# Row numbers of a graph scatter from a scan and two narrow matmuls, and four PSUM banks for the edge rows

## The chip, the cores and the metric

The kernel runs on one core of a Trainium2 chip. The metric is the device time of one execution in microseconds (us). The times are medians over several executions; lower is better.

## The reference, cut to what matters

A graph layer with 6250 nodes of 64 features and 206,250 directed edges (100,000 in both directions and one loop per node), sorted by `dst`. `W1a` to `Wr` are small dense weights, the hidden width is 128.

```
msg  = concat([x[dst], edge_attr], axis=1)          # 206250 x 128
h    = relu(msg @ W1a.T + b1a) @ W1b.T + b1b
sums = segment_sum(h, src, 6250);  counts = segment_sum(1, src, 6250)
agg  = sums / max(counts, 1)
z    = relu(concat([x, agg]) @ W2a.T + b2a) @ W2b.T + b2b
out  = concat([z, x]) @ Wr.T + br
return layernorm(x + out)
```

Edges come in the order of `dst`, but are summed by `src`. Between the two the rows of all edges have to be brought into another order.

## The kernel before

All of the timed work is in `fast_path`. The edges are padded to 1612 tiles of 128 and taken in 124 groups of 13 tiles (`NGR`, `NG`, `BLK`). The nodes are divided into 49 bins of 128 consecutive `src` numbers (`NB`; padded to 50, `2 * HALF`). Each edge row is sent to a place in a DRAM table `rows`, within the region of its bin; later the table is read back bin by bin, and a one-hot matmul sums the rows of each bin. There are five epochs (`EPOCHS`: 82, 17, 14, 7 and 4 groups), each with a table, and within the first one several steps, after which the part of the table that is then full can be read.

One turn of the main loop, `for k, ep_ in enumerate(epoch_of)`, does this, and each step is written for the engines in this order:

1. `group(k + 3)`: SyncE loads edge features (L700), the place of each edge's `dst` in a window (L912), and the window's table `ytab` (L918), into one of four `rhs` buffers.
2. ScalarE copies the low seven bits of `src` into the rows of the group (L1182).
3. `counts_of` (L850, L851) for group k + 1: four TensorE matmuls into two PSUM banks, `cnt_ps`.
4. `hidden(k, ...)` for tiles 0 to 9 in parts of 4, 3 and 3: TensorE multiplies (L949) into an `h_ps` bank, ScalarE applies Relu and writes the rows `orow` (L950; five buffers). An f32 product is two passes in the trace.
5. `columns(k + 2)` (L929) and `bins_of(k + 2)` (L830, L831, L837) on VectorE.
6. In turns 6 to 18, `nodes_ahead` (L1150 to L1160), work of the node layer that needs no sums.
7. `issue(k)`: SyncE reads back parts of the table into one of nine `rt` buffers (`READS`, L1005).
8. `sum_next()`, if sums are due: VectorE makes one-hots of the next reads (L1031, L1034), TensorE multiplies them with the rows (L1050, into one of two `sum_ps` banks), VectorE adds the result to `part` (L1106).
9. `slots(k + 1)` (L867, L872): VectorE writes the row numbers `rowidx` of group k + 1.
10. `hidden(k, ((10, 3),))`, the last three tiles, after the first two sums.
11. `scatter(k)`: GpSimd issues 13 indirect DMAs (L956), each of 128 rows of 130 numbers, to the places that `rowidx` names.

TensorE, VectorE, ScalarE and SyncE run in exactly the order in which the program is written (`manual_schedule`). After the loop the last bins are summed and the node layer follows. GpSimd has no part in that.

How a row number is found before the change: `bins_of` compares the bin number of each edge with 0 to 49, which gives a one-hot of 50 bins x 13 tiles for each partition, with a column 0 ahead of each bin that holds what that partition and bin had up to the previous group (L830). A running sum over it (L837, the scan) numbers the edges within partition and bin; only differences within a bin matter. `counts_of` adds up the 128 partitions: `one_w` sums the counts of all partitions, `before_w` adds those of the partitions below in the same tile, and `BIG` on the diagonal marks the bin that the edge belongs to. `slots` takes the maximum over the 50 bins (L867), which is the marked one, and adds the bin's start (L872).

PSUM has eight banks: one holds the constants `ramp`, `in_win` and `on` that VectorE reads, two are `cnt_ps`, two `sum_ps` and three `h_ps`.

Of the kernel before, what the change touches and what calls it, by code (L numbers as in the profile page):

```python
# [8 lines left out]
F32 = mybir.dt.float32  # L9
# [454 lines left out]
ROWS, EDGES, READS = 5, 4, 9  # L464
# [13 lines left out]
def fast_path(  # L478
# [161 lines left out]
    eye_b = const.tile([P, P], F32, name="eye_b")  # L640
    nc.vector.tensor_scalar(eye_b, diff_i, 0.0, BIG, op0=ALU.is_equal, op1=ALU.mult)
# [36 lines left out]
    with (  # L678
# [6 lines left out]
        tc.tile_pool(name="hps", bufs=3, space=PSUM) as hp,  # L685
# [10 lines left out]
        rhss = [rp.tile([P, NG * P], F32, name=f"rhs{i}") for i in range(EDGES)]  # L696

# [28 lines left out]
        def y_rows(b_lo, b_hi):  # L726
            for b0 in range(b_lo, b_hi, SUB):
                n = min(SUB, b_hi - b0)
                ps = hp.tile([P, SUB, H], F32, name="h_ps")
                for j in range(n):  # L730
                    b = b0 + j
                    nc.tensor.matmul(
                        ps[:, j, :], zT[: D + 1, b * P : (b + 1) * P], w1x_t, start=True, stop=True
                    )
                nc.scalar.copy(part[:, b0 : b0 + n, :H], ps[:, :n, :])
                if b0 + n == NB or (b0 + n) % (4 * SUB) == 0:
                    c0 = b0 // (4 * SUB) * (4 * SUB)
                    nc.scalar.dma_start(yv[:, c0 : b0 + n, :], part[:, c0 : b0 + n, :H])
# [17 lines left out]
        nc.vector.scalar_tensor_tensor(  # L756
            before_w, diff_i, 0.0, eye_b, op0=ALU.is_gt, op1=ALU.add
        )
        state = {"rt": 0, "bad": 3}
# [5 lines left out]
        none_b = const.tile([P, 2 * HALF], BF16, name="none_b")  # L765
        nc.vector.memset(none_b, 0.0)
# [52 lines left out]
        hads = {}  # L819

        def bins_of(k):


            ep_ = epoch_of[k]
            c0 = k * BLK
            oh = slp.tile([P, 2 * HALF * T], BF16, name="bins")
            had = slp.tile([P, 2 * HALF * T], BF16, name="had")
            by_bin = oh.rearrange("p (b t) -> p b t", t=T)
            was = none_b if k == ep_.first else state["had"][:, :, BLK]
            nc.vector.tensor_tensor(by_bin[:, :, 0], was, on.rearrange("p (b t) -> p b t", t=T)[:, :, 1], op=ALU.mult)  # L830
            nc.vector.tensor_tensor(  # L831
                by_bin[:, :, 1:],
                ramp[:, : 2 * HALF, None].to_broadcast([P, 2 * HALF, BLK]),
                hi[:, None, c0 : c0 + BLK].to_broadcast([P, 2 * HALF, BLK]),
                op=ALU.is_equal,
            )
            nc.vector.tensor_tensor_scan(had, on, oh, 0.0, op0=ALU.mult, op1=ALU.add)  # L837
            oh, had = (v.rearrange("p (b t) -> p b t", t=T) for v in (oh, had))
            state["had"] = hads[k] = had
            return oh, had  # L840

        def counts_of(oh, had):

            ps = slpp.tile([P, 2, 512], F32, name="cnt_ps")
            for i in range(2):
                v = ps[:, i, : HALF * T].rearrange("p (b t) -> p b t", t=T)
                b = slice(i * HALF, (i + 1) * HALF)
                nc.tensor.matmul(v, one_w, had[:, b, :], start=True, stop=False)  # L850
                nc.tensor.matmul(v[:, :, :BLK], before_w, oh[:, b, 1:], start=False, stop=True)  # L851
            return ps

        def slots(k, ps):

            ep_ = epoch_of[k]
            c0 = k * BLK
            at = (k - ep_.first) % SEG * BLK
            if at == 0:
                m = min(ep_.end - k, SEG) * BLK  # L860
                state["bin"] = slp1.tile([P, SEG * BLK], F32, name="bin_at")[:, :m]
                nc.vector.tensor_scalar(
                    state["bin"], hi[:, c0 : c0 + m], float(STRIDE), -BIG, op0=ALU.mult, op1=ALU.add
                )
            v = ps[:, :, : HALF * T].rearrange("p i (b t) -> p i b t", t=T)
            row = slp.tile([P, T], F32, name="row")
            nc.vector.tensor_reduce(row, v.rearrange("p i b t -> p t i b"), axis=mybir.AxisListType.XY, op=ALU.max)  # L867

            def by_now(t):
                nc.vector.tensor_copy(t.rearrange("p (i b) -> p i b", i=2), v[:, :, :, BLK])  # L870

            s = nc.vector.scalar_tensor_tensor(  # L872
                rowidx[:, c0 : c0 + BLK], row[:, :BLK], BIG + STRIDE - 1,
                state["bin"][:, at : at + BLK], op0=ALU.min, op1=ALU.add,
            )
            state["slots"] = s.ins
            if k + 1 == EARLY:
                by_now(early)
                wrong(early, epochs[0].low, ALU.is_gt, slp)
            for st in ep_.steps[:-1]:  # L880
                if k + 1 == st.at:
                    full = slp1.tile([P, 2 * HALF], F32, name="full")
                    by_now(full)
                    wrong(full, st.hi, ALU.is_lt, slp)
            if k + 1 == ep_.end:
                by_now(ep_.tot)
                unused(ep_)

                if (ep_.end - ep_.first) * BLK > 255:
                    most = slp.tile([P, 2 * HALF], F32, name="most")  # L890
                    nc.vector.tensor_scalar(
                        most, hads[k][:, :, BLK], 255.5, None, op0=ALU.is_gt, op1=ALU.add,
                        accum_out=bad[:, state["bad"] :][:, :1],
                    )
                    state["bad"] += 1
# [38 lines left out]
        def window(g):  # L934

            ps = hp.tile([P, H], F32, name="h_ps")
            nc.tensor.matmul(ps[D:, :], near[: D + 1, g, :], w1x_t, start=True, stop=True)
            nc.scalar.copy(mv[g % MV][D:, :], ps[D:, :])
# [3 lines left out]
        def hidden(k, parts):  # L942
            orow = orows[k % ROWS]
            rhs, _, m = made[k]
            for k0, n in parts:
                ps = hp.tile([P, SUB, H], F32, name="h_ps")
                for j in range(n):
                    c = k0 + j
                    nc.tensor.matmul(ps[:, j, :], rhs[:, c * P : (c + 1) * P], m, start=True, stop=True)  # L949
                nc.scalar.activation(orow[:, k0 : k0 + n, :H], ps[:, :n, :], AF.Relu)  # L950
# [195 lines left out]
        def nodes_ahead(b0):  # L1146
            n = min(SUB, NB - b0)
            cols = slice(b0 * P, (b0 + n) * P)
            qp = hp.tile([P, SUB * P], F32, name="h_ps")
            nc.tensor.matmul(qp[:, : n * P], w2x_t, zT[: D + 1, cols], start=True, stop=True)  # L1150
            xp = hp.tile([P, 2, SUB, D], F32, name="h_ps")
            for j in range(n):
                b = slice((b0 + j) * P, (b0 + j + 1) * P)
                nc.tensor.matmul(xp[:, 0, j, :], zT[: D + 1, b], wrx_t, start=True, stop=True)  # L1154
            nc.vector.tensor_scalar(nq[:, cols], qp[:, : n * P], -1.0, None, op0=ALU.mult)  # L1155
            nc.scalar.copy(xr[:, b0 : b0 + n, :], xp[:, 0, :n, :])
            for j in range(n):
                b = slice((b0 + j) * P, (b0 + j + 1) * P)
                nc.tensor.matmul(xp[:, 1, j, :], nq[:, b], nwzz_t, start=True, stop=True)  # L1159
            nc.vector.tensor_add(xr[:, b0 : b0 + n, :], xr[:, b0 : b0 + n, :], xp[:, 1, :n, :])  # L1160
# [12 lines left out]
        counts = counts_of(*bins_of(0))  # L1173
        columns(0)
        slots(0, counts)
        for k, ep_ in enumerate(epoch_of):
# [6 lines left out]
            if k == 0:  # L1183
                hidden(k, ((0, 4), (4, 3), (7, 3), (10, 3)))
                window(1)
                columns(1)
                ahead = bins_of(1)
            if k + 1 < NGR:
                counts = counts_of(*ahead)
# [8 lines left out]
            if k + 2 < NGR:  # L1198
                columns(k + 2)
                ahead = bins_of(k + 2)  # L1200
# [17 lines left out]
            if k == 4:  # L1218


                wps = hp.tile([P, P], F32, name="h_ps")
# [3 lines left out]
                wps = hp.tile([P, D], F32, name="h_ps")  # L1225
# [5 lines left out]
                wps = hp.tile([P, H + D], F32, name="h_ps")  # L1231
# [11 lines left out]
            for i in range(max(due, 1)):  # L1243
# [3 lines left out]
                if i == 0 and k + 1 < NGR:  # L1247
                    slots(k + 1, counts)
# [23 lines left out]
        with tc.tile_pool(name="nw", bufs=3) as nw:  # L1272

            class Nodes:
# [17 lines left out]
                def turned(self):  # L1292
                    tr = hp.tile([P, SUMS * P], F32, name="h_ps")
# [5 lines left out]
                def layer(self):  # L1299
                    p1 = hp.tile([P, SUMS * P], F32, name="h_ps")[:, : self.nb * P]  # L1300
# [3 lines left out]
                def residual(self):  # L1304
                    p3 = hp.tile([P, SUMS, D], F32, name="h_ps")
# [65 lines left out]
            bad_ps = slpp.tile([P, NBAD], F32, name="cnt_ps")  # L1371
# [61 lines left out]
```

## Time and profile before

| what | value |
|---|---|
| median of 16 runs | 2555.23 us (2540.46 to 2564.58) |
| the profiled execution | 2554.95 us |
| its span in the trace | 2553.2 us |
| mean granted TensorE clock | 0.718 of full speed |
| scatter L956: instructions, busy | 1612, 1547.8 us |
| first scatter starts, last scatter starts | 17.5 us, 2428.0 us |
| DMA traffic | 375.2 MB, 147 GB/s |

Line numbers (L956) are those of the kernel before. PE is TensorE's matmul, PEld its weight load, DVE is VectorE, ACT ScalarE, POOL GpSimd, and SPq SyncE's DMA queue. A group row of the page gives line, engine, operation, output and inputs, shape and count; then busy us and mean ns of one; then the engine's idle time just before these instructions, with what ended most of it. "issue" is idle time in which the engine waited for nothing that the profile shows; "remote" is a wait whose end the profile can't lay to an instruction of this core.

### The profile page before, as it was taken

To read this page: it belongs to the slowest core of one execution; us is meant where nothing else is said; L and a number is where in the kernel's file an instruction comes from. 1 tells how busy PE (TensorE), PEld (TensorE's weight loads), DVE (VectorE), ACT (ScalarE), POOL (GpSimd) and SP (SyncE) were. 2 spreads that over 40 slices of the span, in tenths; PEclk is the share of its full clock that TensorE was granted. 3 is DMA by queue.
4 is the path that set the end of the run, shared out by engine and by line. 5 is a ranking of instruction groups with operands and counts; after the bars stand their busy time and mean duration, and the time that the engine had idled before them with its cause. 6 is when DMAs were issued, how large, how long until landed. Compare 5 with 4: busy or idle time off the path is not lost.

```text
span 2553.2 us, 25025 instructions
## 1 busy us (share of the span) xinstructions
PE 1442.2 (56%) x8253; PEld 1269.4 (50%) x8253; DVE 1186.9 (46%) x1993; ACT 325.7 (13%) x807; POOL 1555.7 (61%) x1630
## 2 busy tenths in 40 slices
PE   3645462345554554445545566665666565665796
PEld 2534452344444444435444456555555564565795
DVE  5333343333433544333444555464555454554587
ACT  1211110111111111001101001110111100110106
POOL 6666566666666666666666666656666666666500
PEclk7665665666776776667776777777777776787898
DMA  6657554534444444334444444644445454555581
GB/s 162 192 193 263 156 156 127 181 114 127 125 126 126 124 132 116 116 105 128 129 130 121 141 153 148 182 131 133 151 134 169 146 146 141 164 163 158 173 259 37
DMA packets 198783, 375.21 MB, mean 147 GB/s; under 512 B 47098, under 2 KB 113980, under 8 KB 198516
## 3 DMA queue, kind: packets, MB, share of 16 engines
q1 hardware_dynamic: 121314, 223.67, 31.2%
q0 software_dynamic: 51584, 107.40, 13.2%
q10 hardware_dynamic: 25746, 42.45, 4.9%
q8 instruction: 67, 1.10, 0.2%
q14 instruction: 72, 0.59, 0.1%
HBM read 221.77 MB, written 151.59 MB: 146 GB/s over the span
## 4 chain that ended last, share of the span: by engine, by line
PE 20%; issue 12%; another core or an unknown queue 11%; DVE 5%; ACT 1%; SPq 1%; DMA 1%; ACTq 0%; DVEq 0%
PE sum_ps L1050 12%; PE h_ps L949 7%; DVE oh L1034 2%; DVE part L1106 1%; PE cnt_ps L850 1%; PE cnt_ps L851 1%; DVE rhs L929 1%; DMA rhs<-in_edgeT 1%; SPq L1005 1%; DVE had L837 1%; ACT orow L950 0%; ACT agg L1288 0%; DMA rt<-rows 0%; DVE row L867 0%
## 5 line engine op out<-in xcount | busy, mean ns | idle before, releaser
L956 POOL DMA_INDIRECT rows<-orow,rowidx x1612 | 1547.8, 960 | 872.6 <-issue 453.8
L949 PE MATMUL h_ps<-mv,rhs 128*128 128x128 f32 x3224 | 639.5, 349 | 477.2 <-issue 342.0
L949 PEld LDWEIGHTS h_ps<-mv,rhs 128*128 128x128 f32 x3224 | 574.9, 257 | 549.2 <-issue 398.1
L1050 PE MATMUL sum_ps<-rt,oh 128*128 128x129 f32 x4006 | 609.4, 310 | 264.2 <-issue 230.7
L1050 PEld LDWEIGHTS sum_ps<-rt,oh 128*128 128x128 f32 x4006 | 577.0, 225 | 287.1 <-issue 249.6
L950 ACT ACTIVATE orow<-h_ps 128x512 f32<-128x512 f32 x496 | 247.2, 519 | 2043.7 <-remote 1395.5
L1034 DVE TENSOR_TENSOR oh<-ramp,rt 128x512 f32<-128x512 f32 (+3 forms) x213 | 147.4, 704 | 595.1 <-DMA rt<-rows 430.6
L929 DVE TENSOR_TENSOR rhs<-rhs,ramp 64x1664 f32<-64x1664 bf16 x116 | 219.4, 1891 | 28.8 <-DMA rhs<-relt 14.0
L850 PE MATMUL cnt_ps<-had,one_w 128*128 128x350 bf16 x248 | 98.6, 400 | 186.5 <-issue 113.8
L837 DVE TENSOR_TENSOR_SCAN had<-ramp,bins 128x700 bf16<-128x700 bf16 x124 | 200.3, 1615 | 4.2
L1034 DVE TENSOR_TENSOR oh<-ramp,node 128x512 f32<-128x512 f32 (+3 forms) x237 | 187.4, 791 | 8.0
L1106 DVE TENSOR_TENSOR part<-part,sum_ps 128x258 f32<-128x258 f32 (+2 forms) x183 | 86.2, 472 | 214.0 <-remote 153.9
L867 DVE TENSOR_REDUCE row<-cnt_ps 128x14 f32<-128x700 f32 x124 | 109.1, 880 | 111.1 <-remote 64.0
L851 PEld LDWEIGHTS <-before_w 128*128 128x128 bf16 x248 | 28.4, 115 | 210.9 <-issue 199.5
L1031 DVE SCALAR_TENSOR_TENSOR node<-unused,rt 128x4 f32<-128x4 bf16 (+3 forms) x237 | 37.8, 159 | 184.2 <-DMA rt<-rows 125.6
L851 PE MATMUL cnt_ps<-bins,before_w 128*128 128x325 bf16 x248 | 100.7, 408 | 28.3 <-issue 28.3
L831 DVE TENSOR_TENSOR bins<-ramp,hi 128x650 bf16<-128x650 f32 x124 | 108.3, 873 | 0.0
L1155 DVE TENSOR_SCALAR zT<-h_ps 128x512 f32<-128x512 f32 (+1 forms) x13 | 8.6, 661 | 132.8 <-PE h_ps L1154 74.5
L1150 PE MATMUL h_ps<-zT,w2x_t 65*128 65x512 f32 (+1 forms) x26 | 21.7, 931 | 64.4 <-ACT orow L950 53.0
L850 PEld LDWEIGHTS <-one_w 128*128 128x128 bf16 x248 | 29.6, 119 | 56.0 <-issue 45.9
L830 DVE TENSOR_TENSOR bins<-had,ramp 128x50 bf16<-128x50 bf16 x119 | 44.2, 371 | 2.7
L1159 PE MATMUL h_ps<-nwzz_t,zT 128*128 128x64 f32 x98 | 22.3, 402 | 40.6 <-DVE zT L1155 34.9
(113 smaller groups left out, 395.9 us busy)
## 6 DMA issues: line engine op xcount, KB each, us to landing
rt<-rows SPq DMA_DIRECT2D x242, 260.0 KB
rhs<-in_edgeT SPq DMA_DIRECT2D x124, 416.0 KB
rt<-rows SPq DMA_DIRECT2D x106, 390.0 KB
rows<-orow,rowidx POOLq DMA_INDIRECT x1612
rhs<-relt SPq DMA_DIRECT2D x116, 208.0 KB
rows<-padrow ACTq DMA_DIRECT2D x4, 4680.0 KB
rows<-padrow ACTq DMA_DIRECT2D x8, 2340.0 KB
rt<-rows SPq DMA_DIRECT2D x48, 325.0 KB
```

The source lines that it names most:

```text
L831: nc.vector.tensor_tensor(by_bin[:, :, 1:], ramp[:, : 2 * HALF, None].to_broadcast([P, 2 * HALF, BLK]), hi[:, None, c0 : c0 + BLK].to_broa ...
L837: nc.vector.tensor_tensor_scan(had, on, oh, 0.0, op0=ALU.mult, op1=ALU.add)
L850: nc.tensor.matmul(v, one_w, had[:, b, :], start=True, stop=False)
L851: nc.tensor.matmul(v[:, :, :BLK], before_w, oh[:, b, 1:], start=False, stop=True)
L867: nc.vector.tensor_reduce(row, v.rearrange("p i b t -> p t i b"), axis=mybir.AxisListType.XY, op=ALU.max)
L929: nc.vector.tensor_tensor(rhs[D:, :].rearrange("p (h e) -> p h e", h=2), rel, in_win[D:, :, None].to_broadcast([WIN, 2, NG * P // 2]), op= ...
L949: nc.tensor.matmul(ps[:, j, :], rhs[:, c * P : (c + 1) * P], m, start=True, stop=True)
L950: nc.scalar.activation(orow[:, k0 : k0 + n, :H], ps[:, :n, :], AF.Relu)
L956: s = nc.gpsimd.indirect_dma_start(out=ep_.rows, out_offset=bass.IndirectOffsetOnAxis(ap=rowidx[:, t : t + 1], axis=0), in_=orow[:, j, :], ...
L1034: nc.vector.tensor_tensor(res[:, at_tile : at_tile + nb * n, :], ramp[:, None, :].to_broadcast([P, nb * n, P]), node[:, :, None].to_broadc ...
L1050: nc.tensor.matmul(of_bin(b), oh[:, at_tile, :], rt[:, j * n + t, : H + 1], start=t0 + t == st.lo[b], stop=t0 + t == st.hi[b] - 1,)
L1106: nc.vector.tensor_add(to, to, g.ps[:, : g.nb, :])
```

## The change

The row number is put together differently, and PSUM is divided differently.

- `bins_of` writes the one-hot into one of two fixed buffers `ohs`, whose column 0 stays zero. The scan then numbers within partition, bin and group (`nth`). A new 50-column VectorE operation adds the last column to a running count, `had` (L848 of the kernel after).
- `counts_of` is replaced by `bases_of` (L885, L886 after): two matmuls of 50 columns, one that sums the counts of all partitions over the groups before, and one that adds the partitions below in this group. `counted` (L858 after) adds a third matmul in the eleven turns in which the totals are needed.
- `slots` adds `bases` (PSUM) to `nth` (SBUF) over 128 x 650 numbers (L900 after), adds `BIG` where the one-hot is set (L903 after, both inputs in SBUF), takes the maximum over the bins of an SBUF tile (L905 after), and adds the bin's start (L906 after).
- `cnt_ps` becomes one bank. `h_ps` becomes four single banks that `bank()` hands out in turn. The parts of a group stay at 4, 3, 3 and 3 tiles. `nodes_ahead` uses three banks where it used two.
- `READS` goes from 9 to 8. `eye_b` and `none_b` are no longer needed.

```diff
-ROWS, EDGES, READS = 5, 4, 9
+ROWS, EDGES, READS = 5, 4, 8
...
-        tc.tile_pool(name="hps", bufs=3, space=PSUM) as hp,
+        tc.tile_pool(name="hps", bufs=1, space=PSUM) as hp,
...
+        banks = hp.tile([P, 4, 512], F32, name="h_ps")
+        def bank(n=1):
+            i = -(-state["bank"] // n) * n % 4
+            state["bank"] = (i + n) % 4
+            return banks[:, i : i + n, :].rearrange("p i f -> p (i f)")
...
         def bins_of(k):
-            was = none_b if k == ep_.first else state["had"][:, :, BLK]
-            nc.vector.tensor_tensor(by_bin[:, :, 0], was, on.rearrange("p (b t) -> p b t", t=T)[:, :, 1], op=ALU.mult)
             nc.vector.tensor_tensor(
-                by_bin[:, :, 1:],
+                ohs[k % 2][:, :, 1:],
                 ramp[:, : 2 * HALF, None].to_broadcast([P, 2 * HALF, BLK]),
                 hi[:, None, c0 : c0 + BLK].to_broadcast([P, 2 * HALF, BLK]),
                 op=ALU.is_equal,
             )
-            nc.vector.tensor_tensor_scan(had, on, oh, 0.0, op0=ALU.mult, op1=ALU.add)
+            nc.vector.tensor_tensor_scan(
+                nth, on, ohs[k % 2].rearrange("p b t -> p (b t)"), 0.0, op0=ALU.mult, op1=ALU.add
+            )
+            if k == epoch_of[k].first:
+                nc.vector.tensor_copy(had, nths[k][:, :, BLK])
+            else:
+                nc.vector.scalar_tensor_tensor(
+                    had, hads[k - 1], 1.0, nths[k][:, :, BLK], op0=ALU.mult, op1=ALU.add
+                )
...
-            for i in range(2):
-                nc.tensor.matmul(v, one_w, had[:, b, :], start=True, stop=False)
-                nc.tensor.matmul(v[:, :, :BLK], before_w, oh[:, b, 1:], start=False, stop=True)
+        def bases_of(k):
+            if k > 0:
+                counted(k - 1)
+            first_ = k == epoch_of[k].first
+            if not first_:
+                nc.tensor.matmul(bases, one_w, hads[k - 1], start=True, stop=False)
+            nc.tensor.matmul(bases, before_w, nths[k][:, :, BLK], start=first_, stop=True)
...
         def slots(k):
-            nc.vector.tensor_reduce(row, v.rearrange("p i b t -> p t i b"), axis=mybir.AxisListType.XY, op=ALU.max)
+            nc.vector.tensor_tensor(
+                own, bases[:, :, None].to_broadcast([P, 2 * HALF, BLK]), nths[k][:, :, 1:], op=ALU.add
+            )
+            nc.vector.scalar_tensor_tensor(own, ohs[k % 2][:, :, 1:], BIG, own, op0=ALU.mult, op1=ALU.add)
+            nc.vector.tensor_reduce(row, own.rearrange("p b t -> p t b"), axis=mybir.AxisListType.X, op=ALU.max)
...
         def hidden(k, parts):
             for k0, n in parts:
-                ps = hp.tile([P, SUB, H], F32, name="h_ps")
+                ps = bank().rearrange("p (j h) -> p j h", h=H)
```

## The prediction

> **What bounds the kernel now.** I read the engines' busy time first, then the waits of the scatter line, the list of all waits, the timeline of one late stretch, and last the groups that the change touches.
>
> Busy time by engine, from the page (us, share of the span, instructions):
>
> ```profile
> PE 1442.2 (56%) x8253; PEld 1269.4 (50%) x8253; DVE 1186.9 (46%) x1993; ACT 325.7 (13%) x807; POOL 1555.7 (61%) x1630
> ```
>
> No engine is full. POOL leads, and nearly all of it is the 1612 scatters of L956. What this line waits for (idle us, times):
>
> ```profile
>   issue: 453.8, 1456
>   ACT orow L1182: 222.4, 53
>   ACT orow L950: 182.0, 56
> ```
>
> A scatter takes 0.96 us and the next starts 0.30 us later ("issue", 1456 times), so the pace is 1.264 us: 13 per group make 16.43 us, 124 groups 2037 us. The first starts at 17.5 us, the last ends at 2429, and 124 us of nodes follow. What is left, 222.4 + 182.0 = 404 us in 109 waits of some 3.7 us, is POOL waiting for rows that ACT has not written. This is the only large part of the span that the change can reach. Who holds ACT (us, times, longest):
>
> ```profile
> ACT orow L950 <- remote: 1395.5, 128, 25.5
> PE h_ps L949 <- ACT orow L950: 131.5, 20, 25.2
> ```
>
> ACT is idle; it waits for PE's matmuls, mostly with no releaser that the trace can name ("remote"). PE in turn rarely (20 times, and 7 times at L1150, 53.0 us) waits for ACT to empty an h_ps bank. The timeline shows how this comes about (start, us, engine, line; idle before and releaser in brackets):
>
> ```profile
> 1875.41 0.96 POOL L956 DMA_INDIRECT rows<-orow,rowidx  x1 [3.53 <-ACT orow L1182]
> 1878.13 4.24 PE L1050 MATMUL sum_ps<-rt,oh 128*128 128x129 f32 x28
> 1882.20 0.83 PE L949 MATMUL h_ps<-mv,rhs 128*128 128x128 f32 x6
> 1886.24 0.31 PE L850 MATMUL cnt_ps<-had,one_w 128*128 128x350 bf16 x1
> 1890.57 0.96 POOL L956 DMA_INDIRECT rows<-orow,rowidx  x1 [0.30 <-issue]
> ...
> 1893.88 0.42 DVE L1106 TENSOR_TENSOR part<-part,sum_ps 128x258 f32<-128x258 f32 x1 [0.26 <-remote]
> 1893.95 0.48 SPq L700 DMA_DIRECT2D rhs<-in_edgeT  x1
> 1894.01 0.49 ACT L950 ACTIVATE orow<-h_ps 128x384 f32<-128x384 f32 x1 [15.09 <-remote]
> 1894.78 0.95 POOL L956 DMA_INDIRECT rows<-orow,rowidx  x1 [3.25 <-ACT orow L1182]
> ...
> 1896.04 1.04 POOL L956 DMA_INDIRECT rows<-orow,rowidx  x1 [0.31 <-issue]
> ```
>
> The last three tiles of the group, part (10,3), are recorded on PE at 1882.2 to 1883.0, yet ACT gets them at 1894.0, together with SP's load L700 and DVE's L1106: all waiters on PE are released within 0.13 us. POOL's last scatter began at 1890.57 and ended at 1891.53; the release comes 2.5 us later. The same picture returns in most cycles: after POOL restarts, ACT is served promptly for some 3 to 10 us, then nothing of PE reaches anyone until POOL pauses. I do not know the mechanism. I take from it only this: a part that PE finishes early after a restart is served in time; one that it finishes later costs a pause of 3 to 4 us.
>
> **The change part by part.** The profiled execution took 2554.95 us, its span 2553.2 and 1.75 outside it; the median of 16 is 2555.23. I add to 2555. A difference of 0.2%, 5 us, is about what can be told from none.
>
> The groups touched (busy us, mean ns; idle before and its releaser):
>
> ```profile
> L850 PE MATMUL cnt_ps<-had,one_w 128*128 128x350 bf16 x248 | 98.6, 400 | 186.5 <-issue 113.8
> L867 DVE TENSOR_REDUCE row<-cnt_ps 128x14 f32<-128x700 f32 x124 | 109.1, 880 | 111.1 <-remote 64.0
> L831 DVE TENSOR_TENSOR bins<-ramp,hi 128x650 bf16<-128x650 f32 x124 | 108.3, 873 | 0.0
> L830 DVE TENSOR_TENSOR bins<-had,ramp 128x50 bf16<-128x50 bf16 x119 | 44.2, 371 | 2.7
> ```
>
> *PE.* Four matmuls of 350 or 325 columns become two of 50. In the timeline four of them follow each other at 0.15 us (1885.94 to 1886.54 for all), so 0.6 us; in slow stretches (1870.1 to 1871.5, one per 0.7 us) 2.8. The two new ones have no row; between L949's pace of 0.14 us and the slow 0.7 they take 0.3 to 1.4. PE saves 0.3 to 1.4 us per group; I take 0.5, nearer to the quick stretch, since that is where a part can still be in time. The third matmul of counted() comes 11 times in all: nothing.
>
> *Banks.* h_ps goes from three banks to four. Where PE stood before (7,3), it now makes these six passes while ACT is still held: 6 x 0.2 = 1.2 us saved after the release, in 27 of 109 pauses, 0.3 us on average. Added, PE comes to part (10,3) 0.8 us earlier after a restart. The window in which a part is served closes somewhere within 7 us (3 to 10), so 0.8 / 7 = 11% of the pauses would be missed: 0.11 x 404 = 46 us gained. With both at their best (1.2 + 1.4 = 2.6 us) it is 37%, 150 us; if only POOL's pause reopens the path whatever PE did, it is nothing. L1150's stage uses three banks instead of two, as before within those that are there.
>
> *VectorE.* Out: 0.371 + 0.880 = 1.25 us per group. In: the 50-column add (between L1031's 0.16 and L830's 0.37), two 650-column operations like L831 (0.87 each) and a reduce of 650 instead of 700 (0.88 x 650/700 = 0.82), together 2.7 to 2.9. That is 1.55 us more per group, 190 us in all, DVE 46% to 54%. What hides it: row numbers are ready 11 to 34 us before their group's first scatter from the sixteenth group on (end of L872 to first L956), and 4.4 us at the worst before that, but for the first group at 1.7. The first loses about 1.5 us once. Without that cover it would be 190 us.
>
> *A moved wait.* L867 waited for PE after the one-hots of the next sums; now the 50-column add, directly behind the scan, waits for the same PE step (its buffer is what bases_of read), and ahead of it are L1031, L1034, L1106 and the new slot operations. In the timeline's cycle the scan ends at 1890.7 and the release comes at 1894.0: four one-hots that had been made from 1890.63 on would start 3.3 us later. Covered: the first is then ready at 1894.0 + 0.2 + 0.85 = 1895.0, and PE takes up the sums at 1896.0, and DVE makes 14 tiles in 3.3 us while PE takes 14 x 0.3. I put it at nothing; if PE has no parts left to do in that time it costs 1 us or more.
>
> *GpSimd's side.* L903 takes both operands from SBUF, 650 elements. Rows that show what this can do: in the last line of the timeline above a scatter began 0.26 us behind the start of L792, two SBUF operands, 0.46 us long, and took 1.04 instead of 0.96. Nine further L792, and L1031 and L872 beside 266 scatters (0.16 us each), show nothing. L925, one operand but 1.09 us, stretched seven scatters to 1.18 to 1.52. If a scatter waits out L792's kind but for 0.15 us, L903 meets a start with 0.87 / 1.264 = 69%, and then costs (0.72 x 0.72 / 2) / 0.87 = 0.30 us: 0.2 us per group, 25 us. From 0 (the 266) to 0.87 x 124 = 108 us (each one in full). I take 25, by the row nearest in kind and length.
>
> The Trainium skill, "SBUF — State Buffer", under "Who interferes with whom", says that a VectorE instruction with two SBUF inputs contends with a GpSimd instruction that reads SBUF but not with one that only writes, and that descriptor generation by GpSimd should not be held up by a tensor_tensor (marked there as inferred); by the first reading the sum is 2535 or above, by the second 2510, and the one L792 row speaks for the first.
>
> *Reads 9 to 8.* The order of reads on SP's queue, and how many go in each group, stay; only the waits for buffers shift (175 instead of 146 reads wait for PE too). DVE waits 430.6 + 125.6 us for these reads, off POOL's path. Nothing; bounds 10 us either way, a few per cent of those waits. The last 124 us hold no wait for reads and are unchanged.
>
> Sum: 2555 - 46 + 25 + 1.5 = 2535.
>
> **The rivals.**
> *Twice the room.* PE gets (10,3) through in a third of the pauses (2.6 of 7 us): 150 gained, 25 lost: 2430. For it: in the cycle shown, part (10,3) ends 7.6 us after the restart, within the doubtful window. Against: sums of 28 matmuls, 4.2 us, still lie before it.
> *The pause is POOL's own.* Each pause ends 2.5 us after its last scatter; if that drain sets the period, PE's savings give nothing and only the port counts: 2555 + 25 = 2580, or 2555 where the port gives nothing as well.
> *The moved wait decides (slower).* Place: the 50-column add, behind the scan. It decides from the point at which PE, with the fourth bank filled ahead, reaches the sums before DVE has the first one-hot. Then the 3.3 us less the 1.2 that the part (7,3) had covered go to (10,3): 2.1 us later, 2.1 / 7 = 30% of pauses longer by one more, 0.3 x 404 / 2 = 60 us with half the groups in that case, less the 15 that the saved matmuls give back, plus 25 of the port: 2625. For it: in 30 groups PE's step is recorded later than or within 1 us ahead of the end of the scan. Against: in most groups of 400 to 1400 us DVE waits for reads at that place.
>
> **How the numbers follow.** The forecast, 2490 to 2549, has 0.40 and 2535 as its middle; twice the room 0.12; no change (gain and port cancel, or neither acts) 0.10; the pause is POOL's own with the port's loss 0.22; the moved wait 0.16. Faster 0.52, same 0.10, slower 0.38. The range leaves out half of the first rival's side and the far part of the last: 2445 to 2612. The likeliest side by itself is 2490 to 2549.
>
> **What would show it.** Right: fewer than 109 waits at L956, together 340 to 370 us; 1.26 us between scatters but for some 60 to 80 of 1.1 to 1.7 us beside L903; DVE near 1375 us; PE's waits for L950 gone. Wrong: L956's waits unchanged or above 404; scatters over 1 us in none or in most groups; a wait of the 50-column add for PE above 100 us with L1050 waiting for L1034.

## The result, and the profile after

The kernel after took 2668.42 us (median of 11 runs, 2662.95 to 2676.76) against 2553.35 us for the kernel before: ratio 1.0452 with a 95% interval of 1.0434 to 1.0470. It is 115 us slower; the prediction was 2535 us, and even the slower end of its range, 2612, is missed. The profiled execution has a span of 2667.1 us.

The kernel before took 2553 to 2575 us (medians) in some sets of runs (a set is made together, the kernel before among it) and 2148 to 2150 us in others, on one and the same chip too, so every comparison below is with the kernel before in the same set. In the second kind GpSimd hardly pauses: the trace of before has 2 gaps over 0.35 us between scatters there, against 108 in the first trace of before. Both kinds turn out to be useful.

The lines that answer to those of before. Busy time by engine, and the scatter with its idle time, from the page:

```profile
PE 1590.0 (60%) x8011; PEld 1419.5 (53%) x8011; DVE 1448.0 (54%) x2241; ACT 338.2 (13%) x807; POOL 1575.8 (59%) x1630
...
L970 POOL DMA_INDIRECT rows<-orow,rowidx x1612 | 1567.9, 973 | 906.9 <-issue 448.5
...
L905 DVE TENSOR_REDUCE row<-own 128x13 f32<-128x650 f32 x124 | 158.7, 1280 | 4.3
```

The scatter's row of the kernel before:

```profile
L956 POOL DMA_INDIRECT rows<-orow,rowidx x1612 | 1547.8, 960 | 872.6 <-issue 453.8
```

TensorE executes 242 matmuls less and is busy 148 us longer. Scatters are 20 us longer in all, and GpSimd's idle time in front of them grew by 34 us. What L970 and L963 waited for, from the list of all waits (total us, times, longest):

```profile
PE h_ps L963 <- ACT orow L964: 644.1, 235, 10.8
...
POOL rows L970 <- ACT orow L1197: 293.3, 87, 6.7
...
POOL rows L970 <- ACT orow L964: 108.8, 28, 16.7
```

GpSimd waits for ScalarE's rows 402 us, as before (404); the rise of its idle time is in waits put down to VectorE (38 us, under 1 us before). But TensorE's wait for ScalarE, 131.5 us in 20 cases before, has become 644.1 us in 235. The loop shows what kind of wait that is (start, us, engine, line; idle before and releaser):

```profile
1215.86 0.60 ACT L964 ACTIVATE orow<-h_ps 128x512 f32<-128x512 f32 x1 [2.12 <-PE h_ps L963]
...
1216.51 1.65 PE L963 MATMUL h_ps<-mv,rhs 128*128 128x128 f32 x6 [0.75 <-ACT orow L964]
...
1218.26 0.49 ACT L964 ACTIVATE orow<-h_ps 128x384 f32<-128x384 f32 x1 [1.80 <-PE h_ps L963]
...
1218.80 1.65 PE L963 MATMUL h_ps<-mv,rhs 128*128 128x128 f32 x6 [0.64 <-issue]
...
1220.54 0.49 ACT L964 ACTIVATE orow<-h_ps 128x384 f32<-128x384 f32 x1 [1.80 <-issue]
```

Product, eviction (ScalarE's reading of a bank, which frees it), product, eviction: ScalarE ends at 1216.46 and TensorE begins the next part at 1216.51; it ends at 1218.16 and ScalarE begins at 1218.26. One part takes 2.29 us. There are four banks, but the work goes through them as if there were one. The tail says it more plainly. All work from the last scatter on, before (first fence) and after (us of the stretch; busy us of each engine with counts; granted clock, DMA share, GB/s):

```profile
2429.00:2553.00 124.00, 101.66 (x746) 91.16 (x745) 100.83 (x361) 44.72 (x133) 0.00 (x0) 0.93 0.49 152
```

```profile
2484.00:2667.00 183.00, 134.07 (x743) 113.34 (x741) 100.34 (x349) 44.69 (x133) 0.00 (x0) 0.72 0.34 100
```

Nearly the same instructions, and VectorE and ScalarE as busy as before, in 183 us instead of 124. The 115 us are thus 59 in the tail (183.7 against 124.2 from the end of the last scatter) and 54 in the loop (last scatter's end 2483.5 against 2429.0). In the tail too a product into one bank waits for ScalarE to empty another:

```profile
2535.18 0.46 ACT L1314 COPY aT<-h_ps 128x384 f32<-128x384 f32 x1
2535.69 0.30 PEld L1318 LDWEIGHTS h_ps<-aT,wam_t 128*128 128x128 f32 x2 [1.62 <-ACT aT L1314]
2535.69 0.91 PE L1318 MATMUL h_ps<-aT,wam_t 128*128 128x384 f32 x2 [1.38 <-ACT aT L1314]
```

L1318 needs the `aT` of the group before, copied at 2533.25; it waits for the copy of 2535.18, which empties the bank next to its own. Over the whole tail, the weight load of this product waited for that copy (total us, times, longest), before and after:

```profile
PEld h_ps L1301 <- ACT aT L1297: 2.1, 11, 0.3
```

```profile
PEld h_ps L1318 <- ACT aT L1314: 31.8, 16, 2.6
```

My theory from here on (A): because the change makes the four banks slices of one tile, and waits between engines are kept by tile, each product waits for the last eviction from that tile, whatever bank it was in. The rivals: (B) the moved wait of the 50-column add, my forecast's slower rival, which the trace seems to support with 270 us of idle time before L848, though its list of waits has no line in which the sums (L1064) wait for the one-hots (L1048); (C) GpSimd held by the two-operand step L903.

### The profile page after: what moved, and what is told of

Same layout as the page of the kernel before. It is cut to its first block, busy times and chain, and to the rows that moved or that the text cites. A ratio compares the mean times of both kernels' runs of the same rounds, so it can differ in the third digit from the quotient of the medians.

```text
span 2667.1 us, 24907 instructions
## 1 busy us (share of the span) xinstructions
PE 1590.0 (60%) x8011; PEld 1419.5 (53%) x8011; DVE 1448.0 (54%) x2241; ACT 338.2 (13%) x807; POOL 1575.8 (59%) x1630
## 4 chain that ended last, share of the span: by engine, by line
another core or an unknown queue 35%; PE 28%; issue 14%; DVE 9%; ACT 6%; POOL 3%; SPq 3%; DMA 2%; ACTq 0%; DVEq 0%; POOLq 0%
PE h_ps L963 13%; PE sum_ps L1064 9%; ACT orow L964 4%; POOL rows L970 3%; DVE oh L1048 2%; SPq L1019 1%; DMA rows<-orow,rowidx 1%; DVE part L1120 1%; PE h_ps L1325 1%; PE h_ps L739 1%; DVE nth L840 1%; DVE rhs L943 1%; DVE row L905 1%; PE h_ps L1318 1%
## 5 line engine op out<-in xcount | busy, mean ns | idle before, releaser
L970 POOL DMA_INDIRECT rows<-orow,rowidx x1612 | 1567.9, 973 | 906.9 <-issue 448.5
L963 PE MATMUL h_ps<-mv,rhs 128*128 128x128 f32 x3224 | 796.1, 413 | 848.9 <-ACT orow L964 644.1
L963 PEld LDWEIGHTS h_ps<-mv,rhs 128*128 128x128 f32 x3224 | 665.7, 301 | 958.7 <-ACT orow L964 705.5
L1064 PE MATMUL sum_ps<-rt,oh 128*128 128x129 f32 x4006 | 659.9, 336 | 88.0 <-issue 65.1
L1064 PEld LDWEIGHTS sum_ps<-rt,oh 128*128 128x128 f32 x4006 | 644.2, 252 | 102.2 <-issue 76.2
L1048 DVE TENSOR_TENSOR oh<-ramp,rt 128x512 f32<-128x512 f32 (+3 forms) x213 | 146.0, 705 | 307.6 <-DMA rt<-rows 155.2
L840 DVE TENSOR_TENSOR_SCAN nth<-ramp,bins 128x700 bf16<-128x700 bf16 x124 | 200.3, 1615 | 4.3
L1048 DVE TENSOR_TENSOR oh<-ramp,node 128x512 f32<-128x512 f32 (+3 forms) x237 | 187.3, 790 | 8.0
L848 DVE SCALAR_TENSOR_TENSOR had<-had,nth 128x50 bf16<-128x50 bf16 x119 | 29.7, 249 | 270.5 <-remote 166.1
L905 DVE TENSOR_REDUCE row<-own 128x13 f32<-128x650 f32 x124 | 158.7, 1280 | 4.3
L903 DVE SCALAR_TENSOR_TENSOR own<-bins,own 128x650 f32<-128x650 bf16 x124 | 104.0, 838 | 4.3
L900 DVE TENSOR_TENSOR own<-cnt_ps,nth 128x650 f32<-128x650 f32 x124 | 102.6, 827 | 5.1 <-remote 2.6
L885 PE MATMUL cnt_ps<-had,one_w 128*128 128x50 bf16 x119 | 24.8, 208 | 30.8 <-DVE full L865 16.8
L1318 PE MATMUL h_ps<-aT,wam_t 128*128 128x384 f32 (+1 forms) x34 | 20.6, 697 | 27.0 <-ACT aT L1314 26.6
L886 PE MATMUL cnt_ps<-nth,before_w 128*128 128x50 bf16 x124 | 31.0, 250 | 9.4 <-DVE at L782 4.8
L886 PEld LDWEIGHTS <-before_w 128*128 128x128 bf16 x124 | 14.3, 115 | 38.0 <-issue 34.8
```

What stands on the lines that cost most here:

```text
L840: nc.vector.tensor_tensor_scan(nth, on, ohs[k % 2].rearrange("p b t -> p (b t)"), 0.0, op0=ALU.mult, op1=ALU.add)
L900: nc.vector.tensor_tensor(own, bases[:, :, None].to_broadcast([P, 2 * HALF, BLK]), nths[k][:, :, 1:], op=ALU.add)
L903: nc.vector.scalar_tensor_tensor(own, ohs[k % 2][:, :, 1:], BIG, own, op0=ALU.mult, op1=ALU.add)
L905: nc.vector.tensor_reduce(row, own.rearrange("p b t -> p t b"), axis=mybir.AxisListType.X, op=ALU.max)
L970: s = nc.gpsimd.indirect_dma_start(out=ep_.rows, out_offset=bass.IndirectOffsetOnAxis(ap=rowidx[:, t : t + 1], axis=0), in_=orow[:, j, :], ...
L1048: nc.vector.tensor_tensor(res[:, at_tile : at_tile + nb * n, :], ramp[:, None, :].to_broadcast([P, nb * n, P]), node[:, :, None].to_broadc ...
```

## The experiments

**The shared tile.** `four_tiles` is the kernel after with four one-bank tiles:

```diff
-        tc.tile_pool(name="hps", bufs=1, space=PSUM) as hp,
+        tc.tile_pool(name="hps", bufs=4, space=PSUM) as hp,
...
-        banks = hp.tile([P, 4, 512], F32, name="h_ps")
...
+        def bank():
+            return hp.tile([P, 512], F32, name="h_ps")
```

> The kernel after, with h_ps as a pool of four one-bank tiles instead of one tile of four banks; nothing else. Theory A (one tile): in the kernel after every product waits for the eviction of the part just before it, as if there were one bank. Then this edit takes away nearly all of the loss: the part after the last scatter falls from 184 us to about 124, TensorE's idle time before L949's counterpart for ScalarE from 644 us to under 150, total 2530 to 2580 us (20 to 30 us above before may remain from the longer scatters beside the two-operand step). Theory B (the moved wait of the 50-column add behind the scan): nothing of that add is changed, so the loop keeps its length and only the end of the kernel can move: total above 2600 us. Theory C (GpSimd held by the two-operand step): total stays above 2640 us.

`before_one_tile` does the reverse: the kernel before, its three banks cut out of one tile.

```diff
+        banks = hpool.tile([P, 3, 512], F32, name="h_ps")
...
+                v = banks[:, hp.at, :n]
+                hp.at = (hp.at + 1) % 3
```

> The kernel before, with its three h_ps banks as slices of one tile; nothing else. Theory A: it slows down as the kernel after does, the end from 124 us to about 184 and the loop by 30 to 60 us: 2630 to 2680 us. Theories B and C: no change, 2545 to 2565 us.

Measured, in a set in which before took 2148.19 us: `four_tiles` 2173.0 (1.0117, 1.0100 to 1.0133), `before_one_tile` 2210.35 (1.0298, 1.0280 to 1.0315). The absolute numbers of both expectations are off, since before itself was 405 us shorter than I had assumed. Against before, `four_tiles` is where I expected it (25 us over); `before_one_tile` shows the longer tail but not the 30 to 60 us in the loop. One tile costs 62 us, all of it in the tail: the last scatter ends at 2059.4 us, the tail is 147.9 us. With four tiles the tail is 85.4. The kernel before, unchanged, gives 2062.2 and 87.2, and the kernel after 2087.3 and 146.8:

> The kernel before, unchanged, for its trace where the other runs are made. In the first four runs GpSimd never waited for rows: 1612 scatters took 16.4 us per group, and the kernel before took 2148 us, 405 us less than where the two kernels were first compared. 405 us is what its 404 us of waits for ScalarE's rows were there. Expected: last scatter ends near 2060 us, about 85 us of nodes after it, no wait of L956 for ScalarE above 30 us, and ScalarE's 'remote' waits (1395.5 us there) near zero.

> The kernel after, unchanged. If the two costs found (one tile 62 us, two-operand step 24 us) are all there is where GpSimd is never held by late products, it takes 2148 + 62 + 24 = 2234 us, within 10. More than 2245: the moved wait or the buffers of the reads cost as well. Less: the two overlap.

`before_here` took 2151.2 us, a single run, and is as expected: its waits for ScalarE at L956 are 11 us, and ScalarE has no "remote" wait. `after_here` took 2239.76 us (before 2149.98; ratio 1.0420, 1.0403 to 1.0437). 62 + 24 = 86 of its 90 us are accounted for, the 24 by the two-operand step below.

The same reverse edit once more, this time in a set in which GpSimd paused (before 2556.48):

> The kernel before with its three h_ps banks as slices of one tile, once more. Where GpSimd pauses (before near 2570 us): if the shared tile explains the loop too, 90 to 125 us over before, with the last scatter ending 30 to 60 us later; if it explains only the tail, 55 to 65 us over before. Where it does not pause (before near 2150): 62 us again, all in the tail.

> The kernel after, unchanged, beside the others. Where GpSimd pauses: 105 to 120 us over before; where it does not: 90.

`before_one_tile_2` took 2667.95 us (1.0446, 1.0410 to 1.0483), `after_2` 2659.80 (1.0405, 1.0370 to 1.0440). The kernel before with nothing changed but the tile is as slow as the kernel after; its last scatter ends at 2481.2 (2429.0 in the first trace of before), its tail is 183.4 us. That is both parts of the loss. The loop shows how:

```profile
1390.21 2.08 PE L967 MATMUL h_ps<-mv,rhs 128*128 128x128 f32 x8 [7.75 <-ACT orow L968]
1390.43 0.95 POOL L974 DMA_INDIRECT rows<-orow,rowidx  x1 [3.23 <-ACT orow L1200]
...
1392.38 0.60 ACT L968 ACTIVATE orow<-h_ps 128x512 f32<-128x512 f32 x1 [2.12 <-PE h_ps L967]
...
1393.04 1.65 PE L967 MATMUL h_ps<-mv,rhs 128*128 128x128 f32 x6 [0.75 <-ACT orow L968]
...
1395.33 1.65 PE L967 MATMUL h_ps<-mv,rhs 128*128 128x128 f32 x6 [0.64 <-issue]
...
1400.93 0.83 PE L967 MATMUL h_ps<-mv,rhs 128*128 128x128 f32 x6
...
1408.91 0.49 ACT L968 ACTIVATE orow<-h_ps 128x384 f32<-128x384 f32 x1 [11.35 <-remote]
...
1409.68 0.96 POOL L974 DMA_INDIRECT rows<-orow,rowidx  x1 [3.12 <-ACT orow L1200]
```

GpSimd restarts at 1390.43. The three parts of tiles 0 to 9, one after the other with ScalarE between them, last until 1397.0, the sums follow, and part (10,3) comes at 1400.93, 10.5 us after the restart; in the cycle of before that the prediction shows it was 6.8. It is served at 1408.91, after GpSimd has stopped. These two cycles are typical: from a restart to the start of the next part (10,3) the median over all pauses is 5.6 us in the first trace of before, 10.9 here and 11.0 in the kernel after. This kernel pauses 132 times (gaps over 0.35 us between scatters), 107 of them in front of the scatter of tile 10; the first trace of before pauses 108 times, 59 of them there. Beyond the usual 0.30 us the gaps come to 423 us, against 373: that is the loop's loss.

`two_tiles` asks whether it is the tile that counts: four banks as two tiles, used in turn.

```diff
-        banks = hp.tile([P, 4, 512], F32, name="h_ps")
+        banks = [hp.tile([P, 2, 512], F32, name=f"h_ps{i}") for i in range(2)]
...
-            return banks[:, i : i + n, :].rearrange("p i f -> p (i f)")
+            return banks[i % 2][:, i // 2, :]
```

> The kernel after, with its four h_ps banks as two tiles of two banks, used in turn. If a wait goes to the last eviction in the same tile, this is double buffering: the tail after the last scatter falls from 147 us most of the way to 85, to 85 to 110, total 2175 to 2200 us. If a single product or eviction at a time is what the banks allow anyway, it stays near 2240.

In a set with before at 2574.51 it took 2608.75 us (1.0126, 1.0102 to 1.0149): a third of the loss. Its last scatter ends at 2461.1, level with `before_reads8` of the same set (2460.6), its tail is 146.8 us against 121.0. That set was of the kind with pauses, for which I had given no number; the tail (183.7 in the kernel after) comes down six tenths of the way, as the expectation's upper end says for the other kind. The banks are the same four; only the tiles differ. `three_tiles` is the kernel after with three separate tiles, `bufs=3`:

> The kernel after with h_ps as three one-bank tiles, as many as before. Against four_tiles it prices the fourth bank. My prediction gave it 0.3 us per group, some 15 to 20 us in all; if the pause of GpSimd sets the period whatever TensorE does, it is equal to four_tiles within 8 us. Theory A: 2540 to 2600 us. Theory B: the fourth bank is what brings TensorE too early to the sums, so this is faster than four_tiles.

2171.58 us (1.0113, 1.0096 to 1.0129), equal to `four_tiles`: where GpSimd does not pause, a fourth bank is worth nothing. B's expectation, that it would be faster, is not met.

**The moved wait.** `after_add_later` moves the 50-column add from behind the scan to the end of `slots`:

```diff
             nths[k] = nth.rearrange("p (b t) -> p b t", t=T)
+
+        def had_of(k):
             had = slp.tile([P, 2 * HALF], BF16, name="had")
...
+            had_of(k)
```

> The kernel after, with the 50-column add taken from behind the scan to the end of slots, where VectorE waits for the same TensorE step anyway. Theory B (moved wait): faster than after_here by 20 us or more. Theory A: equal to it within 8 us.

> The kernel after with the 50-column add at the end of slots. Where GpSimd pauses: if the moved wait holds back the one-hots and with them the loop, 20 to 50 us faster than after_2; if not, equal within 10. Where it does not pause: 10 us slower than after_2, as measured.

2249.90 us beside `after_here` at 2239.76, and 2662.45 beside `after_2` at 2659.80. Theory B falls in both kinds of set: without the moved wait the kernel is no faster. The wait in front of L848 is real, but VectorE would have waited a little later, in `slots`, for the same TensorE step. That the first of the two is 10 us slower, where I allowed 8, stays unexplained.

**The two-operand step.** `four_tiles` still lost 25 us. Its trace shows the scatter that starts beside L901 (L903 of the kernel after):

```profile
1350.04 0.84 DVE L901 SCALAR_TENSOR_TENSOR own<-bins,own 128x650 f32<-128x650 bf16 x1
1350.16 1.54 POOL L968 DMA_INDIRECT rows<-orow,rowidx  x1 [0.30 <-issue]
```

The scatter ends 0.82 us after VectorE's instruction does (1351.70 and 1350.88). So do the other scatters that L901 held, whenever within it they began: 70 of the 87 scatters over 0.975 us in this trace start within L901 and end 0.83 to 0.84 us behind it. `four_tiles_psum_own` puts the intermediate sum into the free part of the counts bank, in two halves:

```diff
-            nc.vector.scalar_tensor_tensor(own, ohs[k % 2][:, :, 1:], BIG, own, op0=ALU.mult, op1=ALU.add)
+            for i in range(2):
+                b = slice(i * HALF, (i + 1) * HALF)
...
+                nc.vector.scalar_tensor_tensor(
+                    own[:, b, :], ohs[k % 2][:, b, 1:], BIG, own_ps, op0=ALU.mult, op1=ALU.add
+                )
```

> four_tiles, with the sum of base and number kept in PSUM (two halves of 325 columns in the free part of the counts bank), so that the step that adds BIG reads only one operand from SBUF. Theory C's part: the 71 scatters over 0.975 us fall to 15 or fewer and the time falls by the 20 us that GpSimd's busy time rose (1555.7 to 1575.8), or less where a pause swallows it. If the longer scatters cost nothing, the time is that of four_tiles within 8 us; VectorE has two more instructions per group, 0.1 to 0.2 us, which are hidden.

2148.73 us, ratio 1.0005 (0.9995 to 1.0014): the 24 us are gone. Scatters over 0.975 us fall from 87 to 19 (I expected 15 or fewer), seven more than in before; ten of the 19 start within the 50-column add, which reads two SBUF inputs as well. The edit also halves the instruction, but length alone is not the cause: in `four_tiles` 125 scatters start within the maximum (L903 there), 1.28 us with one SBUF input, and 3 are lengthened; in `four_tiles_psum_own` 82 start within the two halves of 0.49 us, and none is. The scatter's rows, of `four_tiles` and then of `four_tiles_psum_own` (busy us, mean ns, idle before):

```profile
L968 POOL DMA_INDIRECT rows<-orow,rowidx x1612 | 1572.8, 976 | 504.1 <-issue 404.3 <-DMA rows<-orow,rowidx 64.4 <-ACT orow L962 26.0
```

```profile
L973 POOL DMA_INDIRECT rows<-orow,rowidx x1612 | 1548.9, 961 | 504.3 <-issue 399.6 <-DMA rows<-orow,rowidx 62.1 <-ACT orow L967 27.9
```

Both were run again, to see them where GpSimd pauses; the set was of the other kind, so they only repeat the first answer: 2172.27 (1.0112, 1.0095 to 1.0129) and 2148.43 (1.0003, 0.9994 to 1.0013).

> The kernel after with four separate tiles, once more. Where GpSimd pauses (before near 2560 us): my prediction's sum, 20 us under before, holds if the fourth bank lets more parts through; if the pause has its own period, 0 to 10 us from before, as the cut version was (ratio 0.998). Where it does not pause: 25 us over before.

> The same with one operand of the two-operand step in PSUM. Where GpSimd pauses: within 12 us of four_tiles_2, since the pauses take up the longer scatters. Where it does not pause: 24 us less, equal to before.

`four_tiles_split` cuts the step into four instructions of 12 or 13 bins, `for b0, b1 in ((0, 13), (13, 25), (25, 38), (38, 50))`. `before_reads8` is before with `READS = 8`, `before_reads8_two_operand` adds an unused step of that kind to it:

```diff
+            extra = slp1.tile([P, 2 * HALF, BLK], F32, name="extra")
+            nc.vector.scalar_tensor_tensor(
+                extra, hads[k][:, :, :BLK], BIG, hads[k][:, :, 1:], op0=ALU.mult, op1=ALU.add
+            )
```

> four_tiles, with the two-operand step cut into four instructions of 156 or 169 columns (0.25 us each) in place of one of 650 (0.84 us). In four_tiles, 87 scatters were over 0.975 us, 29 us more than 0.958 each in sum, and the last scatter ended 25 us later than in before. If a scatter that begins beside such an instruction waits for its end, short ones hold it for hardly any time: sum of the stretch under 10 us and total 2148 to 2156 us. If it is the amount of data from two operands that counts, the stretch stays: 2168 to 2176 us.

> The kernel before with eight buffers for the reads instead of nine; nothing else. My prediction said nothing, within 10 us. 2145 to 2155 us expected; 2165 or more would make it a cost of its own.

> before_reads8, with one more VectorE instruction per group behind the row numbers: 650 columns, both operands from SBUF, its output unused. By the theory of the held scatter it costs 20 to 28 us on top of before_reads8, all of it in scatters of more than 0.975 us; as VectorE's time alone it costs nothing (VectorE would be near 60% busy).

In that set before took 2574.51 us, and the three 2571.85 (0.9983, 0.9959 to 1.0006), 2576.22 (1.0002, 0.9978 to 1.0027) and 2566.78 (0.9958, 0.9942 to 0.9975). Eight buffers cost nothing. `four_tiles_split` is the only run with separate tiles where GpSimd pauses: there too nothing of the loss is left. The step in four pieces leaves 73 scatters over 0.975 us, but beyond 0.958 us each they take 10 us in all, against 29 in `four_tiles` (87 scatters) and 25 in the kernel after (71). So two SBUF inputs hold a scatter, and the length of the one instruction beside it says for how long. They are not the only thing that does: the five scatters of the first trace of before that start within L925, with one SBUF input, took 1.18 to 1.52 us. The added step lengthens 73 scatters by 26 us in sum, as expected, and yet costs nothing where GpSimd pauses: its gaps, counted as above, fall from 400 us in `before_reads8` to 362. My expectation of 20 to 28 us is missed there; that it came out 0.4% below before I can't explain and wouldn't build on.

**All parts first.** `all_parts_first` is `four_tiles_psum_own` with part (10,3) ahead of the sums.

```diff
-                hidden(k, ((0, 4), (4, 3), (7, 3)))
+                hidden(k, ((0, 4), (4, 3), (7, 3), (10, 3)))
...
-                    if k > 0:
-                        hidden(k, ((10, 3),))
```

> four_tiles_psum_own with all four parts of the edge rows ahead of the sums (the fourth bank makes room for it). Where GpSimd is bound by its own 16.4 us per group it is equal to four_tiles_psum_own and to before within 8 us. Where the pause at the tenth tile returns (part (10,3) late behind the sums) it should take away most of that pause: 1.5 to 3 us per group, 150 to 350 us less than before.

> four_tiles_psum_own with all four parts ahead of the sums. Where GpSimd pauses: if part (10,3) behind the sums is what makes it pause, 100 us or more under before; if its own drain sets the period, within 30 us of before. Where it does not pause: equal to before.

2150.12 us without pauses (1.0001), but 2609.31 (1.0204, 1.0167 to 1.0241) with them: 53 us over before, where I had expected 100 or more under it if part (10,3) was the cause, and within 30 of it if not. The order by which I would have removed the pauses leaves 113 of them, up to 11.4 us long and 421 us in sum (108 and 373 us in the first trace of before); 91 of the 113 are now in front of a group's first scatter, against 45. So a late part (10,3) is not by itself what makes GpSimd pause; what does stays open. No version in these runs is faster than before in both kinds of set. `four_tiles_psum_own` is equal to it in one kind, `four_tiles_split` in the other.

## Why the prediction was wrong

*Banks: the step that failed.* "h_ps goes from three banks to four", and from it 1.2 us saved per pause. I took the number of banks from what `bank()` hands out, and never asked which instruction the next product waits for. There was no fourth bank in effect, and not even a second one: instead of a gain of 17 us (0.3 of the 0.8 us) this line alone cost 62 us (no pauses) or 111 (pauses; 2667.95 against 2556.48).

*"The last 124 us hold no wait for reads and are unchanged."* The same mistake: I checked the tail against one edit, the reads, but `turned`, `layer` and `residual` had all moved to `bank()`. The tail went to 184 us.

*The window.* The picture of the pauses held: parts that come late after a restart are served only when GpSimd stops. It gives the direction of the loop's loss, with part (10,3) starting 10.9 us after a restart instead of 5.6 (medians), but not the size: by my rule 5.3 us in a window of 7 would be three quarters of 404, some 300 us, and the loop lost 52. As a device for gains it failed: `all_parts_first_2`. So the rule behind the 46 us was off too, whatever the banks did. The 404 us also contain the usual 0.30 us of each wait; what lies beyond it is 373.

*PE.* The saving of 0.5 us per group shows in no run's time: `four_tiles_psum_own` is at 1.0005, `four_tiles_split` at 0.9983. The 46 us of gain, 1.8% of the time, were not to be had with separate tiles either: where GpSimd pauses, `four_tiles_split` has an interval of 0.9959 to 1.0006.

*GpSimd's side.* The term was right in size and mechanism: 25 us forecast; in the first trace the scatters became 20 us longer in sum (71 over 0.975 us with 24.6 us beyond 0.958 each, where before had 12 with 4.4), and the difference of `four_tiles` and `four_tiles_psum_own` is 24.3 us. What I had not seen is that it counts only where GpSimd does not pause; where it does, as in the sets of the forecast, the added step of `before_reads8_two_operand` cost nothing. Of the two readings that the Trainium skill offered ("SBUF — State Buffer", "Who interferes with whom") the runs support the first: this VectorE instruction with two SBUF inputs held the scatter beside it, which then ended 0.83 us after it.

*VectorE.* Forecast 190 us more, measured 261; 57 of the difference is the reduce at 1.28 us where I had scaled 0.82. It was hidden, as said: `four_tiles_psum_own`, with all of these instructions, takes as long as before.

*Moved wait and reads.* Nothing, as in my sum; the slower rival had the right sign for the wrong reason. The idle time before L848 (270 us) was the warning not to read a long wait as a cost.

## What to carry to other kernels

Several buffers cut out of one tile may count as one buffer: before counting banks, look in the built program or the trace at which eviction each product waits for. When a trace shows strict alternation of two engines with 0.05 to 0.1 us between them, suspect a shared tile before the sizes. And when an allocator is replaced, go through every place that calls it, the stages far from the change above all.

## What the runs showed of the hardware

The same kernel took about 2150 us in some sets and 2553 to 2575 in others, one chip showing both (2148.19 in `before_one_tile`'s set, 2574.51 in that of `two_tiles`). Without pauses the span of before is 17.4 us to the first scatter, 2045 us of scatters at 16.4 to 16.5 us per group, and a tail of 87; with pauses the scatter's 0.96 us and the instructions are the same, but TensorE's results reach the other engines late while scatters run. What decides between the two stays open; no run here switched it.

The tail shows the clock as well: with TensorE stopping 42 times for 0.2 to 2.4 us (18 times in before), the granted clock fell from 0.93 to 0.72, and the same 49 transposes took 0.365 instead of 0.290 us each (means). The Trainium skill, "TensorE: Matmul & The Clock Gate", under "A second HAM failure mode: psum-queue depth-cycling", describes for another kernel that short stops between groups of matmuls make the clock swing between half and full. This trace agrees: from 2542 to 2631 us the granted clock goes back and forth between 0.5 (as at 2549.4 to 2563.0) and 1.0 (2563.1 to 2566.3), where in before it is 1.0 from 2433.0 to 2542.3 but for 3.4 us. How much of the 59 us is the clock's part, no run separates.
